# An LSTM over 512 steps: rows of x put into another basis by GpSimd, and one addition of 384 columns for a product's left sums

## The chip, the core and the metric

The kernel runs on one core of a Trainium2 chip. TensorE (PE) multiplies, with its weight loads (PEld) shown apart; VectorE (DVE) and ScalarE (ACT) do the elementwise work; GpSimd (POOL) does some elementwise work and issues some transfers; SyncE (SP) issues most of the transfers. The metric is the device time in microseconds (us), and it is compared as the median of several runs.

## The reference

For 32 sequences of 512 steps with 512 features, the output is `x + lstm(x)`:

```
xW = x @ Wx + b                       # 512 features -> 4 gates of 512
a = xW[t] + prev_h @ Wh
i, f, o = sigmoid(a[0]), sigmoid(a[1]), sigmoid(a[2]);  g = tanh(a[3])
next_c = f * prev_c + i * g
next_h = o * tanh(next_c)
```

All of it is float32. `prev_h @ Wh` must be done step after step. `x @ Wx` does not depend on the state and can be done ahead of the steps that use it.

## The kernel before, in words

**Rows.** Eight steps make a row: `load_row` (L321) brings a row of x into a tile of 128 partitions by 8 steps by 4 feature chunks by 32 sequences, over SP's queue. There are 64 rows. Seven buffers take them in turn.

**A step.** `h_part` (L870) multiplies the state with Wh in 64 matmul instructions and adds into two PSUM banks that already hold xW of that step. `cell` (L901) then runs on ACT and DVE: sigmoids and tanh (L911 to L913), the new c (L914 to L916), tanh of it (L917), h (L918) and its transposition `ht` (L919), for which the next step's `h_part` waits. While the cell runs, PE works on products for later rows of `x @ Wx`.

**x @ Wx by fast products.** Rows are taken in groups of four (`NSB` = 14 groups, rows 6 to 61) and multiplied by a scheme of 26 products of sums, in place of 32 products. An operand of such a product on the left is either a half row itself or a "node", which DVE makes from rows and other nodes (`make`, L509; the addition is at L512). Each of these products is done by an inner scheme with 2 by 2 blocks and seven block products. A left block is `a(g, e)`: `g` the earlier or later four steps, `e` one of two feature chunks. Four of the seven need a left sum, which DVE makes with four additions of 128 columns (`push_sums`, L498; additions at L540 to L543): products 5, 6, 7 and 3. Products 1, 2 and 4 take a block as it is (`left`, L545). The first rows (1 to 3) are done by the inner scheme alone, with the same four additions in `inner_sums` (L442, at L446 to L449), rows 4 and 5 by a scheme of 14, and the last two rows again by the inner scheme alone.

**Windows.** Each step has one window `v`. In order of the program: `h_part`; `announce`, which describes the jobs (products) of the next five windows; `evacuate` and `run_due`, which put ACT's and DVE's work on the results into their queues; `products(v)`, which gives PE the inner products of several jobs (five or six of them in a window on the average); `fetch(v)`, which issues the loads for later windows; `load_xw(k + 3)` on POOL's queue; `cell`; and the copies of xW into PSUM (`seed_first` L855 and `seed_last` L861, whose copies are at L859 and L865). `run_due` (L466) picks DVE's elective work from a list with due windows: an entry that is not due yet goes in only where its columns plus 160 fit into the room of the window. A due entry goes in regardless.

**xW on its way.** ACT first fills a buffer with the bias (`fill_bias`, copy at L832). POOL then issues a transfer that adds xW from DRAM to it (`load_xw`, L836), and one step later ACT copies it into PSUM. After each cell, POOL adds x to h for the output (`put_step`, L977).

**What sets the order around the change.** POOL has one queue: for a step, the transfer of L836 and then the addition of L977, which waits for `ht`. DVE has one queue: the window's evacuations, sums and nodes come ahead of the cell's operations. The rows of a group are loaded in four consecutive windows, eight windows ahead of the group. A buffer of a node is free again when the last product that reads it has been issued, by `job.release` in `products` (L588), at inner product 4.

Of the kernel before, what the change touches and what calls it, by code (L numbers as in the profile page):

```python
# [14 lines left out]
P = 128  # L15
# [267 lines left out]
def kernel(  # L283
# [155 lines left out]

    def inner_sums(a, s):  # L442

        v = nc.vector
        return [s[:, g] for g in range(4)], [
            lambda: v.tensor_add(s[:, 0], a(1, 0), a(1, 1)),  # L446
            lambda: v.tensor_sub(s[:, 1], s[:, 0], a(0, 0)),
            lambda: v.tensor_sub(s[:, 2], a(0, 0), a(1, 0)),
            lambda: v.tensor_sub(s[:, 3], a(0, 1), s[:, 1]),  # L449
        ]  # L450

    def block(src):

        return lambda g, e: src[:, 4 * g : 4 * g + 4, e]
# [30 lines left out]
    def node(sb, v):  # L485

        if v < 2 * sb.scheme.mo:
            return raw_block(sb.row + v // 2, v % 2)
        return nodes[sb, v]

    def node_done(sb, v):
        if v < 2 * sb.scheme.mo:
# [5 lines left out]
    def push_sums(job, sb, n):  # L498
        mo, a_ops, a_of = sb.scheme.mo, sb.scheme.a_ops, sb.scheme.a_of

        def want(v):
            if v < 2 * mo or (sb, v) in node_uses:
                return
            how, a, b = a_ops[v - 2 * mo]
            want(a)
            want(b)
            node_uses[sb, v] = sb.scheme.node_uses[v]

            def make():  # L509
                dst = nodes[sb, v] = node_free.pop(0)  # L510
                fn = nc.vector.tensor_add if how == "add" else nc.vector.tensor_sub
                fn(dst, node(sb, a), node(sb, b))  # L512
# [11 lines left out]
        s = job.sums = [None] * 4  # L524

        def push_sum(i, fn):
            def go():
                s[i] = spool.tile([P, 4, B], F32, name=f"s{i}_{sb.at}_{n}", tag=f"s{i}", bufs=(4, 6, 4, 4)[i])
                fn(nc.vector, block(node(sb, a_of[n])))

            push(
                job.w + i,
                P,
                go,
                lambda v: v + 1 >= job.w + i
                and (a_of[n] < 2 * mo or (sb, a_of[n]) in nodes)
                and (i % 2 == 0 or s[i // 2] is not None),
            )

        push_sum(0, lambda v, a: v.tensor_add(s[0], a(1, 0), a(1, 1)))  # L540
        push_sum(1, lambda v, a: v.tensor_sub(s[1], s[0], a(0, 0)))
        push_sum(2, lambda v, a: v.tensor_sub(s[2], a(0, 0), a(1, 0)))
        push_sum(3, lambda v, a: v.tensor_sub(s[3], a(0, 1), s[1]))  # L543

    def left(a, s, sums):  # L545
        if s in (1, 2, 4):
            return a(*{1: (0, 0), 2: (0, 1), 4: (1, 1)}[s])
        return sums[{5: 0, 6: 1, 7: 2, 3: 3}[s]]

# [38 lines left out]
    def products(v):  # L588
        for late, ss in ((4, (4,)), (2, (7,)), (0, (1,)), (1, (6,)), (0, (5,)), (1, (5,)), (3, (2, 3))):
            job = jobs.get(v - late)  # L590
            for s in ss if job and job.w < LATE_AT[0] else ():
                if s != 5 or job.w5 == v:
                    product(job, s)
                if s == 4:
                    job.release()
        for late, parts in enumerate(LATE_PLAN):
            job = jobs.get(v - late)
            for s, part in parts if job and job.w >= LATE_AT[0] else ():
                product(job, s, part)
                given[0] += 1  # L600
# [399 lines left out]
    def prepare(v):  # L1000

        job = jobs.get(v)
        ops = []
        if job is None or job.w >= PAIR_AT:
            return ops
        i, j = job.kind
        for k in range(2):
            if (i, k) not in head_sums:
                if (i, 0) not in head_sums:
                    both = spool.tile([P, 2, 4, 4, B], F32, name=f"s_h{i}", tag="sums", bufs=2)  # L1010
                head_sums[i, k], more = inner_sums(block(raw_block(i, k)), both[:, k])
# [15 lines left out]
    def describe_half(job, h, js):  # L1027
        row = LATE_ROW + 1
        if not late_half:

            def begin():
                f = free.pop(0).rearrange("p k (g t b) -> p k g t b", g=8, t=2)
                for k in range(2):
                    made, more = inner_sums(half_block(raw_block(row, k), h), f[:, k, 0:4])
# [4 lines left out]
            for m in range(8):  # L1039
                push(  # L1040
                    job.w - 3 + m / 4,
                    P // 2,
                    lambda m=m: begin() if m == 0 else half_ops.pop(0)(),
                    lambda v, m=m: v >= job.w - 3 and (len(half_ops) == 8 - m or m == 0),
                )
        job.factors = lambda s: half_factors(row, h, js, late_half)(s)
        job.finish = finish_late(job, row, (h, js))
# [3 lines left out]
    def describe_late(job, j):  # L1051
        def make(i):
            def begin():
                if not late_pairs:
                    assert len(node_free) == NODES
                    node_free.clear()
                    late_pairs.extend(node_pairs)
                tt_[i] = late_pairs.pop(0).rearrange("p m t e b -> p (m t e b)").rearrange("p (n c) -> p n c", c=C)
                ops.extend(t_sums(i))
                ops.pop(0)()  # L1060

            ops = []
# [13 lines left out]

        if isinstance(j, tuple):
            describe_half(job, *j)
            return
        for i in (j, NJ + j):  # L1080
            if i not in RESIDENT:
                make(i)
        if job.w == LATE_AT[0]:

            def both():
                f = free.pop(0).rearrange("p k (g t b) -> p k g t b", g=4, t=4)
                for k in range(2):
                    head_sums[LATE_ROW, k], more = inner_sums(block(raw_block(LATE_ROW, k)), f[:, k])
                    late_ops.extend(more)
                late_ops.pop(0)()  # L1090

            for m in range(8):
                push(
                    job.w - 2 + m / 4,
                    P,
                    lambda m=m: both() if m == 0 else late_ops.pop(0)(),
                    lambda v, m=m: v >= job.w - 2 and (len(late_ops) == 8 - m or m == 0),
                )
# [7 lines left out]
    def describe(job, sb, n):  # L1106
# [10 lines left out]
        job.factors = lambda q: [(left(block(node(sb, left_of)), q, job.sums), right(q))]  # L1117
        job.finish = finish_product(job, sb, n)
        job.release = lambda: node_done(sb, left_of)
        push_sums(job, sb, n)  # L1120

    again = [i for i in range(8) if i not in RESIDENT][1::2]

    def fetch(v):

# [21 lines left out]
            load_row(PAIR_ROW + v - NJ)  # L1147
        if rest < MO and 0 <= sb < NSB:
            load_row(HEAD // ROW + MO * sb + ROWS_AT[rest])

    with tc.manual_schedule():
        warm = work.tile([P, G, P], F32, name="warm", tag="s")
        nc.scalar.activation(warm[:, 0], c_init, AF.Sigmoid)
        for m in range(10):
# [124 lines left out]
```

## Time and profile before

| what | value |
| --- | --- |
| median of 3 runs | 3079.63 us (3079.49 to 3079.68) |
| span of the profiled execution | 3077.3 us |
| around the span (median less span) | 2.3 us |
| PE busy | 3069.2 us |
| DVE busy | 2284.0 us |
| ACT busy | 1981.0 us |
| POOL busy | 810.4 us |
| granted TensorE clock | 1.000 |

The page gives the busy time of each engine first, then the span in 40 slices, the transfers, the chain of work that ended last, and groups of instructions. A group's row has the line, engine and operation, the tiles (out<-in) with their shapes and its count, then its busy time, the mean nanoseconds of one, and the engine's idle time just before them with what ended it. A row of the timeline has the start, the duration, the engine, the line, the operation and the tiles, and in brackets the idle time of the engine before it.

### The profile page before, as it was taken

The page shows a single profiled execution, that of the slowest core. Times are in us where ns is not written, and L with a number is a line of the kernel's source. Part 1 is how long each engine was busy: PE and PEld are TensorE (multiplying, and loading weights), DVE is VectorE, ACT ScalarE, POOL GpSimd, SP SyncE. Part 2 cuts the span into 40 slices and gives each one's busy share as a digit, 9 for nine tenths or more (in the row PEclk, how much of TensorE's full clock was granted, in tenths as well). Part 3 has the DMA queues.
Part 4 walks back from the last instruction along what each step waited for, and adds up shares of the span by engine and source line. Part 5 has one row for each costly group of instructions (what it writes and reads, how often), then busy time and mean ns, then how long its engine had stood idle before and what let it go on. Part 6 is the DMA issues. An engine that isn't in the chain of part 4 may idle for free.

```text
span 3077.3 us, 133753 instructions
## 1 busy us (share of the span) xinstructions
PE 3069.2 (100%) x56612; PEld 1978.0 (64%) x56612; DVE 2284.0 (74%) x6445; ACT 1981.0 (64%) x5724; POOL 810.4 (26%) x1013
## 2 busy tenths in 40 slices
PE   9999999999999999999999999999999999999999
PEld 5555555556666666666666666666666666666666
DVE  6766777777777777777777777777777777777754
ACT  2566666666666666666666666766666666666665
POOL 0122222222222222222222222222222222222331
PEclk9999999999999999999999999999999999999999
DMA  9898898988879888898888988889898898988763
GB/s 318 239 261 214 229 255 224 249 225 235 248 212 263 229 239 242 211 266 211 258 224 216 264 224 252 224 220 263 216 260 225 226 258 221 256 225 219 196 120 71
DMA packets 350647, 708.34 MB, mean 230 GB/s; under 512 B 45792, under 2 KB 118880, under 8 KB 349536
## 3 DMA queue, kind: packets, MB, share of 16 engines
q1 hardware_dynamic: 277616, 568.41, 56.3%
q0 software_dynamic: 72000, 131.10, 26.8%
q8 instruction: 445, 7.29, 1.0%
q14 instruction: 154, 1.26, 0.1%
q10 hardware_dynamic: 432, 0.27, 0.0%
HBM read 513.88 MB, written 185.73 MB: 227 GB/s over the span
## 4 chain that ended last, share of the span: by engine, by line
PE 99%; DVE 1%; DMA 0%; ACT 0%; issue 0%; ACTq 0%; DVEq 0%
PE gates L874 53%; PE acc L579 17%; PE pp L579 17%; PE p L579 6%; PE gates L888 4%; PE gates L786 1%; PE pp L786 0%; PE acc L786 0%; DMA row<-in_x_dram 0%; DVE t L760 0%; DVE c L941 0%; DVE fc L945 0%; DVE fc L939 0%; DVE ht L949 0%; DVE nodes L367 0%
## 5 line engine op out<-in xcount | busy, mean ns | idle before, releaser
L874 PE MATMUL gates<-wh_sb,ht 128*32 128x384 f32 (+1 forms) x30144 | 1723.1, 379 | 0.0
L874 PEld LDWEIGHTS gates<-wh_sb,ht 128*32 128x32 f32 x30144 | 1022.7, 110 | 704.5 <-issue 624.0
L977 POOL TENSOR_TENSOR oc<-xr,ht 128x128 f32<-128x128 f32 x509 | 385.8, 758 | 2225.9 <-DVE ht L919 2045.7
L836 POOL DMA_DIRECT2D xw<-xw x500 | 440.0, 880 | 24.3 <-ACT xw L832 4.8
L911 ACT ACTIVATE s<-gates 128x256 f32<-128x256 f32 x472 | 181.3, 384 | 344.2 <-PE gates L874 333.4
L832 ACT COPY xw<-bias_sb 128x512 f32<-128x512 f32 x500 | 316.1, 632 | 0.0
L579 PE MATMUL pp<-wb,nodes 128*32 128x256 f32 x3920 | 312.3, 379 | 0.0
L914 DVE TENSOR_TENSOR fc<-s,c 128x128 f32<-128x128 f32 x471 | 136.9, 291 | 183.4 <-ACT s L911 180.5
L623 ACT COPY pp<-pu 128x512 f32<-128x512 f32 x396 | 238.7, 603 | 52.9 <-DVE t L744 25.8
L918 DVE TENSOR_TENSOR fc<-s,ig 128x128 f32<-128x128 f32 x472 | 137.7, 292 | 177.4 <-ACT ig L917 177.4
L625 DVE TENSOR_TENSOR pp<-acc,p 128x256 f32<-128x256 f32 x396 | 169.2, 427 | 118.8 <-ACT pp L624 118.6
L913 ACT ACTIVATE s<-gates 128x128 f32<-128x128 f32 x472 | 130.9, 277 | 147.2 <-PE gates L874 147.1
L859 ACT COPY gates<-xw 128x384 f32<-128x384 f32 x468 | 221.2, 473 | 5.4 <-DVE nodes L802 5.4
L579 PE MATMUL pp<-wb,s 128*32 128x256 f32 x2656 | 211.5, 379 | 0.0
L579 PE MATMUL acc<-wb,s 128*32 128x256 f32 x2656 | 211.5, 379 | 0.0
L579 PE MATMUL acc<-wa,s 128*32 128x256 f32 x2656 | 211.5, 379 | 0.0
L579 PE MATMUL p<-wa,s 128*32 128x256 f32 x2656 | 211.4, 379 | 0.0
L917 ACT ACTIVATE ig<-c 128x128 f32<-128x128 f32 x472 | 146.2, 310 | 100.7 <-DVE c L916 62.5
L624 ACT COPY pp<-acc 128x256 f32<-128x256 f32 x396 | 143.3, 362 | 91.0 <-DVE t L744 41.2
L618 DVE TENSOR_TENSOR pu<-acc,p 128x256 f32<-128x256 f32 x396 | 164.5, 415 | 44.3 <-ACT p L615 35.4
L919 DVE STREAM_TRANSPOSE ht<-fc 128x128 f32<-128x128 f32 x472 | 147.0, 311 | 50.3 <-DVE fc L918 1.4
L615 ACT COPY p<-p 128x256 f32<-128x256 f32 x396 | 150.5, 380 | 39.9 <-PE p L579 37.8
(239 smaller groups left out, 4478.6 us busy)
## 6 DMA issues: line engine op xcount, KB each, us to landing
wb<-keep_b SPq DMA_DIRECT2D x332, 512.0 KB, 6.2
xw<-xw POOLq DMA_DIRECT2D x500, 256.0 KB, 5.6
wa<-keep_a SPq DMA_DIRECT2D x332, 384.0 KB, 5.3
xw<-t SPq DMA_DIRECT2D x420, 128.0 KB, 4.0
xw<-raw_sb SPq DMA_DIRECT2D x272, 128.0 KB, 4.0
xr<-in_x_dram SPq DMA_DIRECT2D x256, 128.0 KB, 5.4
out_dram<-oc SPq DMA_DIRECT2D x255, 128.0 KB, 4.3
row<-in_x_dram SPq DMA_DIRECT2D x63, 512.0 KB, 8.2
```

The lines of the kernel that those rows point to most:

```text
L579: nc.tensor.matmul(dst[t * B : (t + 1) * B], a[:, t % a.shape[1]], w[t // a.shape[1]] if isinstance(w, list) else w, start=s in (1, 5) and ...
L615: nc.scalar.copy(job.p5, p5[:, 0])
L618: nc.vector.tensor_add(job.pu[:, 1], job.acc, job.p5)
L623: nc.scalar.copy(job.pp[0], job.pu)
L625: nc.vector.tensor_add(job.pp[1][:, 1], job.acc, job.p5)
L832: nc.scalar.copy(xw[t], bias_sb)
L836: nc.gpsimd.dma_start(out=xw[t], in_=stored[i][a], accum_op=mybir.AluOpType.add)
L859: nc.scalar.copy(gates[t % 2][:, 0:IFG], xw[t][:, 0:IFG])
L874: nc.tensor.matmul(g[j * B : (j + 1) * B, cols], state["ht"][:, k, :], wh_sb[:, k, j, cols], start=False, stop=True, skip_group_check=True,)
L911: nc.scalar.activation(s[:, 0:2], g[:, 0:2], AF.Sigmoid)
L919: nc.vector.transpose(ht.rearrange("p q b -> p (q b)"), h)
L977: (nc.gpsimd if t < T - 3 else nc.vector).tensor_add(state["oc"][:, tt % 2], xr[t][:, tt % 2], ht)
```

## The change

A row is put into another basis in place, once, by three subtractions of GpSimd, two windows after its load has been issued. The earlier half's first chunk stays. The other three blocks become what products 7, 6 and 3 need on the left. Products 5, 4 and 2 then need a sum, and all three sums have one term in common: the block (1, 1) of the new basis. For a node, which is now stored with its two chunks one after the other, they are one addition of 384 columns with that term repeated. For a half row they are one of 256 columns and one of 128. The nodes are sums of rows in the new basis, so that they are in the new basis, too.

```
+    def change_basis(i, a=0, b=ROW):
+        h = (b - a) // 2
+        low, high = (rows[i][:, t : t + h].rearrange("p t (k e) b -> p t k e b", e=2) for t in (a, a + h))
+        sub = nc.gpsimd.tensor_sub
+        sub(high[:, :, :, 0], low[:, :, :, 0], high[:, :, :, 0])
+        sub(high[:, :, :, 1], high[:, :, :, 1], high[:, :, :, 0])
+        sub(low[:, :, :, 1], low[:, :, :, 1], high[:, :, :, 1])
+
+    def inner_sums(src, d):
+        h = src.shape[1] // 2
+        first = src[:, :, 0].rearrange("p (g t) b -> p g t b", g=2)
+        base = src[:, h:, 1]
+        return d, [
+            lambda: nc.vector.tensor_add(d[:, 0:2], base.unsqueeze(1).to_broadcast([P, 2, h, B]), first),
+            lambda: nc.vector.tensor_add(d[:, 2], base, src[:, 0:h, 1]),
+        ]
...
+        def make_sums():
+            d = job.sums = spool.tile([P, 3, 4, B], F32, name=f"d_{sb.at}_{n}", tag="d", bufs=6)
+            if left_of < 2 * mo:
+                for op in inner_sums(node(sb, left_of), d)[1]:
+                    op()
+            else:
+                flat = node_flat(sb, left_of)
+                nc.vector.tensor_add(
+                    d.rearrange("p i t b -> p i (t b)"),
+                    flat[:, 3 * P :].unsqueeze(1).to_broadcast([P, 3, P]),
+                    flat[:, 0 : 3 * P].rearrange("p (i c) -> p i c", i=3),
+                )
+        push(
+            job.w,
+            3 * P,
+            make_sums,
+            lambda v: v + 1 >= job.w and (left_of < 2 * mo or (sb, left_of) in nodes),
+        )
...
     def left(a, s, sums):
-        if s in (1, 2, 4):
-            return a(*{1: (0, 0), 2: (0, 1), 4: (1, 1)}[s])
-        return sums[{5: 0, 6: 1, 7: 2, 3: 3}[s]]
+        if s in (1, 7, 3, 6):
+            return a(*{1: (0, 0), 7: (1, 0), 3: (0, 1), 6: (1, 1)}[s])
+        return sums[:, {5: 0, 4: 1, 2: 2}[s]]
...
-                if s == 4:
+                if s == 3:
                     job.release()
...
+    turned, changed = {}, {1, 2}
...
+        for i in turned.pop(v, ()):
+            change_basis(*i)
+        for i in list(rows):
+            if i not in changed and i:
+                changed.add(i)
+                turned.setdefault(v + 2, []).append((i, 0, ROW // 2) if i == NROWS - 1 else (i,))

     with tc.manual_schedule():
+        change_basis(1)
+        change_basis(2)
```

The last part of `fetch(v)` is where the subtractions are issued, and `load_xw` follows it on POOL's queue. Row 0 keeps its basis, and of row 63 only the first four steps change theirs; the steps left out are multiplied with Wx directly. The sums of the last two rows are pushed in four pieces, where it was eight.

More of the change, by code (lines that the diff above doesn't have):

```diff
@@ L438, in push_factors @@
             push(2 + (FACTORS_TO - 2) * i // len(ops), columns, go, lambda _, i=i: len(done) == i)
[L442 to L449, printed above, removed]
+    def change_basis(i, a=0, b=ROW):
[12 more added lines that the diff above has]
+            lambda: nc.vector.tensor_add(d[:, 2], base, src[:, 0:h, 1]),
         ]
@@ L488, in node, with node_flat @@
             return raw_block(sb.row + v // 2, v % 2)
-        return nodes[sb, v]
+        return node_flat(sb, v).rearrange("p (e t b) -> p t e b", e=2, t=ROW)
+    def node_flat(sb, v):
+        return nodes[sb, v].rearrange("p t e b -> p (t e b)")
     def node_done(sb, v):
@@ L509, in make @@
             def make():
-                dst = nodes[sb, v] = node_free.pop(0)
+                nodes[sb, v] = node_free.pop(0)
                 fn = nc.vector.tensor_add if how == "add" else nc.vector.tensor_sub
-                fn(dst, node(sb, a), node(sb, b))
+                fn(node(sb, v), node(sb, a), node(sb, b))
                 node_done(sb, a)
@@ L523, in push_sums @@
         want(a_of[n])
[L524 to L543, printed above, removed]
+        left_of = a_of[n]
+        def make_sums():
[16 more added lines that the diff above has]
+        )
     def left(a, s, sums):
-        if s in (1, 2, 4):
-            return a(*{1: (0, 0), 2: (0, 1), 4: (1, 1)}[s])
-        return sums[{5: 0, 6: 1, 7: 2, 3: 3}[s]]
+        if s in (1, 7, 3, 6):
+            return a(*{1: (0, 0), 7: (1, 0), 3: (0, 1), 6: (1, 1)}[s])
+        return sums[:, {5: 0, 4: 1, 2: 2}[s]]
     jobs = {}
@@ L1009, in prepare @@
                 if (i, 0) not in head_sums:
-                    both = spool.tile([P, 2, 4, 4, B], F32, name=f"s_h{i}", tag="sums", bufs=2)
-                head_sums[i, k], more = inner_sums(block(raw_block(i, k)), both[:, k])
+                    both = spool.tile([P, 2, 3, 4, B], F32, name=f"s_h{i}", tag="sums", bufs=2)
+                head_sums[i, k], more = inner_sums(raw_block(i, k), both[:, k])
                 ops += more
@@ L1033, in begin @@
                 for k in range(2):
-                    made, more = inner_sums(half_block(raw_block(row, k), h), f[:, k, 0:4])
+                    made, more = inner_sums(raw_block(row, k)[:, 4 * h : 4 * h + 4], f[:, k, 0:3])
                     late_half.append(made)
@@ L1037, in begin @@
                 half_ops.pop(0)()
-            for m in range(8):
+            for m in range(4):
                 push(
-                    job.w - 3 + m / 4,
-                    P // 2,
+                    job.w - 3 + m / 2,
+                    P // (1 + m % 2),
                     lambda m=m: begin() if m == 0 else half_ops.pop(0)(),
-                    lambda v, m=m: v >= job.w - 3 and (len(half_ops) == 8 - m or m == 0),
+                    lambda v, m=m: v >= job.w - 3 and (len(half_ops) == 4 - m or m == 0),
                 )
@@ L1087, in both @@
                 for k in range(2):
-                    head_sums[LATE_ROW, k], more = inner_sums(block(raw_block(LATE_ROW, k)), f[:, k])
+                    head_sums[LATE_ROW, k], more = inner_sums(raw_block(LATE_ROW, k), f[:, k, 0:3])
                     late_ops.extend(more)
                 late_ops.pop(0)()
-            for m in range(8):
+            for m in range(4):
                 push(
-                    job.w - 2 + m / 4,
-                    P,
+                    job.w - 2 + m / 2,
+                    2 * P // (1 + m % 2),
                     lambda m=m: both() if m == 0 else late_ops.pop(0)(),
-                    lambda v, m=m: v >= job.w - 2 and (len(late_ops) == 8 - m or m == 0),
+                    lambda v, m=m: v >= job.w - 2 and (len(late_ops) == 4 - m or m == 0),
                 )
@@ L1116, in describe @@
         left_of = sb.scheme.a_of[n]
-        job.factors = lambda q: [(left(block(node(sb, left_of)), q, job.sums), right(q))]
+        job.factors = lambda q: [(left(lambda g, e: block(node(sb, left_of))(g, e), q, job.sums), right(q))]
         job.finish = finish_product(job, sb, n)
```

## The prediction

> **What bounds the kernel now.** I read the page's busy times and its chain first, then busy time by stage, then single steps in the timeline.
>
> ```profile
> PE 3069.2 (100%) x56612; PEld 1978.0 (64%) x56612; DVE 2284.0 (74%) x6445; ACT 1981.0 (64%) x5724; POOL 810.4 (26%) x1013
> PE 99%; DVE 1%; DMA 0%; ACT 0%; issue 0%; ACTq 0%; DVEq 0%
> ```
>
> The chain of work that ended last is PE for 99% of the span. A busy PE need not be one that works without a pause, so the next view is single instructions of a step of five products (PE, then the end of its cell on DVE, then PE's weight loads), and the end of the cell before a step of six.
>
> ```profile
> 1505.00 0.64 PE L579 MATMUL pp<-wb,nodes 128*32 128x256 f32 x8
> 1505.43 0.64 PE L579 MATMUL acc<-wb,s 128*32 128x256 f32 x8
> ...
> 1506.72 0.64 PE L579 MATMUL p<-wa,s 128*32 128x256 f32 x8
> 1507.15 0.53 PE L874 MATMUL gates<-wh_sb,ht 128*32 128x384 f32 x4
> ```
>
> ```profile
> 1506.40 0.31 DVE L919 STREAM_TRANSPOSE ht<-fc 128x128 f32<-128x128 f32 x1
> ```
>
> ```profile
> 1506.94 0.37 PEld L874 LDWEIGHTS gates<-wh_sb,ht 128*32 128x32 f32 x8
> ```
>
> ```profile
> 1494.31 0.31 DVE L919 STREAM_TRANSPOSE ht<-fc 128x128 f32<-128x128 f32 x1
> ```
>
> ```profile
> 1495.29 0.37 PEld L874 LDWEIGHTS gates<-wh_sb,ht 128*32 128x32 f32 x8
> ```
>
> Products follow one another every 0.43 us, and the step's own matmuls begin 0.43 us after the last product: no pause. In this step `ht` is ready at 1506.71 and its first weight load begins at 1506.94, so the recurrence has a slack of 0.23 us. In the longer step it is 0.67 (1494.62 to 1495.29). PE sets the pace, but the cell is close behind.
>
> ```profile
> 0.00:100.00 100.00, 98.39 (x1636) 52.31 (x1640) 67.85 (x148) 31.90 (x87) 6.07 (x11) 1.00 0.85 293
> 100.00:2800.00 2700.00, 2700.00 (x50041) 1741.42 (x50037) 2051.40 (x5680) 1779.91 (x5023) 731.19 (x906) 1.00 0.86 237
> ```
>
> ```profile
> 3060.00:3077.30 17.30, 11.24 (x204) 7.40 (x196) 7.55 (x35) 5.75 (x28) 0.45 (x1) 0.97 0.06 17
> ```
>
> These are busy times by stage (stretch, its length, then PE, PEld, DVE, ACT, POOL, the granted clock). The clock is full, and between 100 and 2800 us PE is never idle. In the whole span it is idle for 3077.3 - 3069.2 = 8.1 us, 1.6 of them in the first 100 and 6.1 in the last 17, where the last cells have no products beside them.
>
> **The change part by part.** PE's work stays: the same seven products, blocks and columns, with other operands on the left. So a saving elsewhere gains at most the 8.1 us of idle PE, while anything that comes too late is lost in full.
>
> *DVE's sums.*
>
> ```profile
> L540 DVE TENSOR_TENSOR s<-nodes 128x128 f32<-128x128 f32 x261 | 81.7, 313 | 0.1
> ...
> L543 DVE TENSOR_TENSOR s<-nodes,s 128x128 f32<-128x128 f32 x261 | 72.6, 278 | 0.0
> L512 DVE TENSOR_TENSOR nodes<-row,nodes 128x512 f32<-128x512 f32 x99 | 65.3, 659 | 0.1
> L540 DVE TENSOR_TENSOR s<-row 128x128 f32<-128x128 f32 x117 | 33.6, 287 | 0.0
> ...
> L543 DVE TENSOR_TENSOR s<-row,s 128x128 f32<-128x128 f32 x117 | 33.0, 282 | 0.0
> ```
>
> Four additions take about 4 x 0.29 = 1.17 us. Between 128 columns (0.29) and 512 (0.66), 384 come to 0.54 and 256 to 0.41. Sums of nodes: 261 x (1.17 - 0.54) = 164 us. Sums of rows: 117 x (1.17 - 0.41 - 0.29) = 55. DVE loses some 219 us, 0.46 in each of 472 steps, and comes down to 2065, 67% of the span. On the path this is 0, because DVE holds up no PE between 100 and 2800. The trace has no addition with a repeated operand: it takes between 0.54 (as a plain one) and 1.17 us (no gain); I take 0.54, since the columns are the same in number. The nodes' additions keep their 512 columns: 0.
>
> *GpSimd's subtractions.* 63 rows by three; 56 rows belong to the 14 groups. Each has 256 columns, of which the trace shows no example; its 128 columns are these, beside DVE:
>
> ```profile
> 1517.86 0.65 DVE L744 TENSOR_TENSOR t<-t,pp 128x512 f32<-128x512 f32 x1
> ```
>
> ```profile
> 1518.03 0.45 POOL L977 TENSOR_TENSOR oc<-xr,ht 128x128 f32<-128x128 f32 x1 [4.17 <-DVE ht L919]
> ```
>
> ```profile
> 201.70 0.60 POOL L977 TENSOR_TENSOR oc<-xr,ht 128x128 f32<-128x128 f32 x1 [4.86 <-DVE ht L919]
> ```
>
> ```profile
> 201.70 0.28 DVE L541 TENSOR_TENSOR s<-s,nodes 128x128 f32<-128x128 f32 x1
> 201.90 0.55 DVE L540 TENSOR_TENSOR s<-row 128x128 f32<-128x128 f32 x1
> ```
>
> Beside L744, which reads PSUM, it took 0.45. In the second case it waited for L541, and then L540 took 0.55 where its like takes 0.28: the two engines exclude each other, and POOL held DVE for 0.27 us. So 256 columns keep DVE out for 0.27 (if that is a fixed cost) to 0.54 us (by columns), and take 0.45 to 0.45 + 0.27 = 0.72. I take 0.54 and 0.72: DVE's own additions grow with their columns, from 0.29 to 0.66. A row then costs POOL 2.2 us, and up to 3.3 with 0.36 more for each wait behind DVE (0.81 against 0.45, below); DVE can be held 3 x 0.54 = 1.6 us.
>
> The cover of that: DVE's idle time ahead of the cell, what the sums free, and PE's slack.
>
> ```profile
> L914 DVE TENSOR_TENSOR fc<-s,c 128x128 f32<-128x128 f32 x471 | 136.9, 291 | 183.4 <-ACT s L911 180.5
> ```
>
> That is 183.4 / 471 = 0.39 + 0.46 + 0.23 = 1.08 us in the short step, 1.52 in the long one. DVE works 67% of the time, so the hold is 0.67 x 1.6 = 1.07 us a row, and less, because beside an operation that reads PSUM (L744 above) POOL needed no more than its 0.45. So the mean row is just covered. What remains is the row whose subtractions meet the cell itself, where only the slack helps. In each group one row lands late:
>
> ```profile
> 1512.42 0.50 SPq L324 DMA_DIRECT2D row<-in_x_dram  x1
> ```
>
> ```profile
> DMA to landing us min/median/max: 8.2/8.2/8.2
> ```
>
> It was issued at 1512.42 and landed at 1520.6, and POOL would have turned to it after the addition at 1518.03. Its subtractions would run from 1520.6 to 1522.8, with the cell. There only the slack covers. One hold of 0.54 is 0.31 more than the short step's slack and less than the long one's; half and half that is 0.15 us, for 14 groups **2.1 us**. Bounds: 0, and 56 x (1.6 - 1.08) = 29 us.
>
> *Moved past on POOL's queue: the transfer of xW, and x + h.*
>
> ```profile
> 1500.88 0.81 POOL L977 TENSOR_TENSOR oc<-xr,ht 128x128 f32<-128x128 f32 x1 [4.52 <-DVE ht L919]
> 1501.63 0.88 POOL L836 DMA_DIRECT2D xw<-xw  x1
> ```
>
> ```profile
> 1511.49 0.47 ACT L859 COPY gates<-xw 128x384 f32<-128x384 f32 x1
> ```
>
> ```profile
> DMA to landing us min/median/max: 3.8/5.6/9.1
> ```
>
> ```profile
> L911 ACT ACTIVATE s<-gates 128x256 f32<-128x256 f32 x472 | 181.3, 384 | 344.2 <-PE gates L874 333.4
> ```
>
> xW is issued at 1501.63 and first read at 1511.49, 9.86 us later; a transfer lands after 5.6 (median) to 9.1. It is now issued 2.2 to 3.3 us later in 56 steps, so the median still lands in time (8.9), and the slowest is late by up to 2.5. In the row that lands late POOL also waits for it until 1520.6, with this transfer behind it on its queue: 2.6 us more, 11.5 after the usual issue at the median and 1.6 late. Behind ACT's copy on its queue stand the evacuations of the next window, for which DVE waits. ACT has 344.2 / 472 = 0.73 us idle ahead of its sigmoid, and PE 0.23 of slack; most of the lateness ends there. I take **1 us** in all, by the median: 14 such rows at 1.6 - 0.73 - 0.67 = 0.2 would be 2.8 in long steps, and some of ACT's work behind the copy is not waited for. Bounds: 0, and a bad case: with the slower half of the landings evenly spread from 5.6 to 9.1, those over 9.86 + 0.96 - 3.3 = 7.5 are too late even for ACT's idle time and the slack, 0.23 of all and by 0.8 on the average: 56 x 0.23 x 0.8 = 10 us. The addition of x to h (L977) starts a few tenths late at worst, since POOL's step is 0.8 + 3.3 + 0.9 = 5.0 of 5.6 us; only the output waits for it: 0.
>
> *The start.* Row 1 is changed ahead of the first sums.
>
> ```profile
> L324 SPq DMA_DIRECT2D row<-in_x_dram x1: 787/787/787, 10.5 to 10.5; - x1
> ...
> DMA to landing us min/median/max: 9.0/9.0/9.0
> ```
>
> ```profile
> 19.76 0.28 DVE L446 TENSOR_TENSOR s_h<-row 128x128 f32<-128x128 f32 x1
> ```
>
> ```profile
> 20.85 1.05 PE L579 MATMUL p<-t,s_h 128*32 128x256 f32 x16
> ```
>
> Row 1 lands at 19.5, and DVE reads it at 19.76. Now two subtractions (1.44) stand between, and the third can hold DVE for its 0.54: the first sum begins at 21.5 and ends at 21.9, so PE's product begins at about 22.0, 1.15 later; its second half needs the sum of the row's other half, and waits some 0.3 more. That is **1.5 us**, and nothing hides it, since PE's next work stands behind that product. Bounds: 0 (two subtractions of 0.45 and a sum of 0.41 end at 20.8) and 2.7 (three of 1.08, 0.41 for the sum, and the 0.3).
>
> *The rest.* Buffers of nodes come free one window earlier (at product 3): no later than before, 0. Fewer pieces for the last two rows: PE's idle 6.1 us there are the cell's own chain, with no sums in it: 0.
>
> **Sum.** 0 + 2.1 + 1 + 1.5 = 4.6 us on the profiled execution's span of 3077.3, so 3081.9; with the 2.3 us around the span, 3084.2 against the median of 3079.63. About 0.2%, 6.2 us, is what a measurement of this kernel tells from no change. The forecast lies within it.
>
> **The rivals.** *The subtractions hold up the cell (slower).* Place: DVE ahead of L914 in the 56 steps. If DVE is shut out for the whole operation of POOL, a row holds 0.67 x 3 x 0.72 = 1.45 us, 0.37 above the cover of 1.08: 56 x 0.37 = 21 us, with the start and xW 3103. It decides from (6.2 - 2.5) / 56 = 0.07 us a row above the cover. For it: the slack of 0.23. Against it: at 201.90 L540 ended at 202.45, having taken its 0.28 from 202.17, and POOL ended at 202.30, so the hold ended 0.13 earlier. The Trainium skill, page "SBUF — State Buffer", section "Who interferes with whom", says that whoever of VectorE with two inputs in SBUF and GpSimd starts first keeps the shared pair for the whole instruction, while the other is fully blocked. The trace agrees on the blocking and shows a shorter hold; by that rule the time is this rival's. Chance 0.20.
>
> *xW comes late (slower).* The upper bound of 10 us in place of 1: 3079.6 + 1.5 + 2.1 + 10 = 3093. For it: 0.8 us between the slowest landing and its reader. Against it: the median has 4.3. Chance 0.14.
>
> *The sums are not shorter.* If an addition of 384 columns took 1.17 us, nothing would be freed, the cover would be 0.62, and 56 x (1.07 - 0.62) = 25 us would be added to 1.5 and 1: 3107. Chance 0.04.
>
> *Faster.* Shorter sums at the start (four operations for eight) and less DVE work at the end could take back the 1.5 us and a little of the idle PE: some 3078. More than 0.2% would need 6.2 of the 8.1 us, most of them in the last 17 us, where the cell's own chain stands. Chance 0.03.
>
> **How the numbers follow.** Forecast 0.55, the three slower rivals 0.38, other stalls of the two close queues 0.04, faster 0.03. So within 0.2% 0.55, slower 0.42, faster 0.03. The range reaches from just below no change, 3079, to the first rival, 3103; inside it lies the second, outside the third and the worse halves of the others. The forecast's own range is 3080 to 3086.
>
> **What would show it.** DVE's busy time near 2065 and longer operations beside POOL's; POOL's three subtractions near 0.72 each when alone; PE's product after the first sums at 22.0; PE idle or behind 0.43 us a product only in some of the 56 steps. Wrong would make it: subtractions of over 1 us, many weight loads of L874 that wait for `ht`, or ACT's L859 waiting for the transfer in many steps.

## The result, and the profile after

The median rises from 3079.59 us (3079.49 to 3079.68) to 3093.73 us (3093.24 to 3093.94): 14.1 us, a ratio of 1.0046 with a 95% interval of 1.0032 to 1.0060. The span of the profiled execution grows from 3077.3 to 3091.8 us. The kernel has become slower by 0.46%. This is inside the range of the prediction, but the forecast of 3084.2 was 9.5 us too low, and "within 0.2%" was wrong.

From the page of the kernel after, the busy times and the chain by engine:

```profile
PE 3072.9 (99%) x56612; PEld 2020.5 (65%) x56612; DVE 2182.7 (71%) x5408; ACT 1981.1 (64%) x5724; POOL 950.4 (31%) x1202
...
PE 95%; DVE 2%; DMA 2%; SPq 0%; ACT 0%; issue 0%; POOL 0%; DVEq 0%
```

DVE lost 101 us of work, and yet its share of the chain grew from 1% to 2%. Busy time by stage of the kernel after (columns as in the prediction):

```profile
0.00:100.00 100.00, 97.03 (x1600) 51.08 (x1604) 67.09 (x133) 30.39 (x83) 21.46 (x25) 1.00 0.85 293
100.00:2800.00 2700.00, 2690.46 (x49796) 1775.29 (x49792) 1944.85 (x4666) 1772.76 (x5002) 849.74 (x1070) 1.00 0.86 235
...
3060.00:3091.80 31.80, 25.74 (x468) 17.38 (x460) 14.18 (x66) 12.26 (x58) 1.84 (x4) 0.97 0.09 27
```

Between 100 and 2800 us, where PE was never idle before, it is now idle for 9.5 us. The end is unchanged: 6.1 us idle, as before. The clock is the same.

To see where in those 2700 us, one can take, for each of the 472 steps, the start of its first matmul of `h_part` after, less the same start before. The difference is flat for long stretches and rises at few places:

```
step   before    after    after less before
   0     46.67    48.60    1.93
  57    425.67   428.53    2.86   (+0.92)
 248   1554.21  1562.10    7.89
 249   1560.25  1569.08    8.83   (+0.94)
 440   2688.62  2702.20   13.57
 441   2694.67  2709.18   14.52   (+0.94)
 471   2871.65  2886.28   14.62
```

There are thirteen rises of 0.92 to 1.03 us, at steps 57, 89, 121 and so on to 441, one in every 32 steps, which is one in each group of four rows but the last. Thirteen by 0.94 is 12.2 us; the start has 1.93; three small rises (0.25, 0.11, 0.11) make the rest. A cost of the subtractions would come with the rows, four times in 32 steps, or with the one row that lands late. This comes once, and at a step in which GpSimd changes no row. DVE in the window ahead of step 249, from the timeline of the kernel after:

```profile
1562.33 0.28 DVE L458 TENSOR_TENSOR d<-row 128x128 f32<-128x128 f32 x1
1564.31 0.43 DVE L638 TENSOR_TENSOR pp<-acc,p 128x256 f32<-128x256 f32 x1 [1.70 <-ACT pp L637]
1564.65 1.22 DVE L773 TENSOR_TENSOR t<-t,raw_sb 128x1024 f32<-128x1024 f32 x1
1565.89 1.23 DVE L773 TENSOR_TENSOR t<-t,t 128x1024 f32<-128x1024 f32 x1
1567.04 0.28 DVE L927 TENSOR_TENSOR fc<-s,c 128x128 f32<-128x128 f32 x1
...
1568.62 0.31 DVE L932 STREAM_TRANSPOSE ht<-fc 128x128 f32<-128x128 f32 x1
```

and PE at its end:

```profile
1569.08 0.53 PE L887 MATMUL gates<-wh_sb,ht 128*32 128x384 f32 x4 [0.73 <-DVE ht L932]
```

The same window in the timeline of the kernel before:

```profile
1554.50 0.28 DVE L540 TENSOR_TENSOR s<-row 128x128 f32<-128x128 f32 x1
1556.41 0.43 DVE L625 TENSOR_TENSOR pp<-acc,p 128x256 f32<-128x256 f32 x1 [1.64 <-ACT pp L624]
1556.76 1.22 DVE L760 TENSOR_TENSOR slot<-slot,t 128x1024 f32<-128x1024 f32 x1
1557.89 0.28 DVE L914 TENSOR_TENSOR fc<-s,c 128x128 f32<-128x128 f32 x1
...
1559.48 0.31 DVE L919 STREAM_TRANSPOSE ht<-fc 128x128 f32<-128x128 f32 x1
1559.71 1.18 DVE L760 TENSOR_TENSOR slot<-t,slot 128x1024 f32<-128x1024 f32 x1
```

In both, DVE waits some 1.7 us for ACT. In the kernel before, one addition of 1024 columns then comes ahead of the cell, and the second follows behind `ht`; in the kernel after, two come ahead of it. The cell begins 1.48 us after the start of L625 before, and 2.73 us after the start of L638 after: 1.25 more. The recurrence's slack takes some 0.3 of them, and the step's start is late by the other 0.94. PE's idle 0.73 is not all of that: the rows of a product last 0.64 us, while the next matmuls otherwise start 0.43 after that product's start (both in the prediction's rows), so 0.21 of the pause counts as busy.

The pattern is the same in all thirteen windows: two additions of 1024 columns stand directly ahead of the cell there, and in no other step, and in no step of the kernel before. The chain's 2% of DMA are mostly pieces of 4 to 5 us in these windows, where the page's chain goes back from the first L773 to a transfer of weights. DVE did not wait for it: in each of the thirteen the first L773 starts 0.34 us after L638, as L458 starts 0.34 after an L457 of the same 256 columns (in the timeline further below).

Why two? `run_due` takes an entry that is not due yet where its columns plus 160 fit into the room of the window. As the code charges them, this window had 4300 - 672 (a node) - 3 x 288 (the sums that fall into it) - 416 (an evacuation) = 2348 left before, and so had the other twelve. One addition of 1024 columns is charged 1184, two are charged 2368: the second missed by 20. The three sums have become one entry of 384 columns at 544, so 2668 are left, and the second fits. The wait for ACT isn't charged at all. That is theory A: the time that the sums freed was spent again by the planner, in a window that has it only on paper. Theory B, in the expectations below, is that GpSimd's subtractions cost the time.

### The profile page after: what moved, and what is told of

Same layout as the page of the kernel before. It is cut to its first block, busy times and chain, and to the rows that moved or that the text cites. A ratio compares the mean times of both kernels' runs of the same rounds, so it can differ in the third digit from the quotient of the medians.

```text
span 3091.8 us, 132991 instructions
## 1 busy us (share of the span) xinstructions
PE 3072.9 (99%) x56612; PEld 2020.5 (65%) x56612; DVE 2182.7 (71%) x5408; ACT 1981.1 (64%) x5724; POOL 950.4 (31%) x1202
## 4 chain that ended last, share of the span: by engine, by line
PE 95%; DVE 2%; DMA 2%; SPq 0%; ACT 0%; issue 0%; POOL 0%; DVEq 0%
PE gates L887 51%; PE acc L592 17%; PE pp L592 16%; PE p L592 5%; PE gates L901 4%; DMA wb<-keep_b 1%; DMA wa<-keep_a 1%; DVE t L773 1%; PE gates L799 0%; DVE raw_sb L773 0%; SPq L341 0%; DMA row<-in_x_dram 0%; DVE slot_h L773 0%; PE acc L799 0%; PE pp L799 0%
## 5 line engine op out<-in xcount | busy, mean ns | idle before, releaser
L887 PEld LDWEIGHTS gates<-wh_sb,ht 128*32 128x32 f32 x30144 | 1048.5, 110 | 692.1 <-issue 590.9
L990 POOL TENSOR_TENSOR oc<-xr,ht 128x128 f32<-128x128 f32 x509 | 375.6, 738 | 2031.1 <-DVE ht L932 1873.2
L592 PE MATMUL pp<-wb,d 128*32 128x256 f32 x5312 | 427.7, 379 | 0.0
L592 PE MATMUL acc<-wa,nodes 128*32 128x256 f32 x3920 | 294.0, 379 | 0.0
L638 DVE TENSOR_TENSOR pp<-acc,p 128x256 f32<-128x256 f32 x396 | 169.3, 427 | 141.0 <-ACT pp L637 138.9
L592 PEld LDWEIGHTS pp<-wb,d 128*32 128x32 f32 x5312 | 193.9, 110 | 39.8
L592 PE MATMUL p<-wa,d 128*32 128x256 f32 x2656 | 214.0, 379 | 0.0
L592 PEld LDWEIGHTS acc<-wa,nodes 128*32 128x32 f32 x3920 | 154.0, 110 | 58.4
```

The source lines that it names most:

```text
L592: nc.tensor.matmul(dst[t * B : (t + 1) * B], a[:, t % a.shape[1]], w[t // a.shape[1]] if isinstance(w, list) else w, start=s in (1, 5) and ...
L638: nc.vector.tensor_add(job.pp[1][:, 1], job.acc, job.p5)
L887: nc.tensor.matmul(g[j * B : (j + 1) * B, cols], state["ht"][:, k, :], wh_sb[:, k, j, cols], start=False, stop=True, skip_group_check=True,)
L990: (nc.gpsimd if t < T - 3 else nc.vector).tensor_add(state["oc"][:, tt % 2], xr[t][:, tt % 2], ht)
```

## Experiments

### At most one long addition ahead of its time

The kernel after, in `run_due`:

```
-        i = spent = 0
+        i = spent = long = 0
...
-            if window > v and (columns + FIXED > room - spent or not ready(v)):
+            if window > v and (columns + FIXED > room - spent or (columns > 4 * P and long) or not ready(v)):
...
             spent += columns + FIXED
+            long += columns > 4 * P
```

> The changed kernel, but one call of run_due takes at most one operation of more than 512 columns that is not due yet. This moves the second addition of 1024 columns out of 13 windows, one in each group but the last, and changes nothing else on DVE's list but the two entries behind it. Theory A (the cheaper sums leave 2668 columns of room where 2348 were left, so that a second addition of 1024 columns, 1.2 us, goes in ahead of the cell): the 13 delays of 0.94 us go, 3093.7 - 12.2 = 3081.5. Theory B (GpSimd's subtractions hold DVE or make xW late): the subtractions are all there, so 3093 to 3094.

Measured: 3082.15 us (3081.03 to 3083.37), against 3079.37 before on the same chip; ratio 1.0009 (1.0000 to 1.0018). All thirteen rises are gone; by the same comparison of starts, 1.93 at step 0 and 0.27 at step 181 are left (the profiled execution was the fastest of ten, 3081.03). DVE in the same window of this kernel:

```profile
1558.45 0.43 DVE L639 TENSOR_TENSOR pp<-acc,p 128x256 f32<-128x256 f32 x1 [1.71 <-ACT pp L638]
1558.79 1.22 DVE L774 TENSOR_TENSOR t<-t,raw_sb 128x1024 f32<-128x1024 f32 x1
1559.93 0.28 DVE L928 TENSOR_TENSOR fc<-s,c 128x128 f32<-128x128 f32 x1
```

The cell is back where it was, 1.48 us after the start of L639. GpSimd's subtractions are all still there, so they are not what cost the 12 us.

### The kernel before, with 20 columns more room

```
-ROOM = 4300
+ROOM = 4320
```

> The kernel before, with ROOM at 4320 in place of 4300 and nothing else. The room left in the same 13 windows is then 2368, just what two additions of 1024 columns are charged. Theory A: a second one goes in, the cell is held up 13 times by 0.9 us or a little less, since four short sums stand in its DVE list where the changed kernel has one or two: 3079.6 + 9 to 12 = 3089 to 3092, with no work of GpSimd in it. Theory B: no change, 3079.6.

Measured: 3091.56 us (3091.40 to 3091.66); ratio 1.0039 (1.0024 to 1.0054). Thirteen rises of 0.92 to 1.09 us at the same steps, 12.4 in all. Here nothing of the change is in the kernel: four short sums, no subtraction, POOL busy for 818.2 us. DVE's timeline in this kernel, and PE's:

```profile
1562.09 0.43 DVE L625 TENSOR_TENSOR pp<-acc,p 128x256 f32<-128x256 f32 x1 [1.63 <-ACT pp L624]
1562.43 1.22 DVE L760 TENSOR_TENSOR slot<-slot,t 128x1024 f32<-128x1024 f32 x1
1563.68 1.23 DVE L760 TENSOR_TENSOR slot<-t,slot 128x1024 f32<-128x1024 f32 x1
1564.82 0.28 DVE L914 TENSOR_TENSOR fc<-s,c 128x128 f32<-128x128 f32 x1
```

```profile
1566.86 1.50 PE L874 MATMUL gates<-wh_sb,ht 128*32 128x384 f32 x16 [0.73 <-DVE ht L919]
```

The same picture as in the changed kernel, down to PE's 0.73 us. Twenty columns of room are enough to make the loss, and one long addition less is enough to take it away: theory A is shown from both sides.

### The sums alone

The kernel after, with the subtractions left out (the sums then take operands in the old basis):

```
     def change_basis(i, a=0, b=ROW):
...
-        sub(high[:, :, :, 0], low[:, :, :, 0], high[:, :, :, 0])
-        sub(high[:, :, :, 1], high[:, :, :, 1], high[:, :, :, 0])
-        sub(low[:, :, :, 1], low[:, :, :, 1], high[:, :, :, 1])
+        return
```

> The changed kernel without GpSimd's subtractions: the rows keep their basis, so that the products take wrong operands on the left and the output is not the reference's; the rest is the same. Theory A: the 13 delays stay, and only the start (1.9 us) and some 0.4 us of other delays go: 3091.4. Theory B: nothing holds DVE, 3079.6 to 3080.

Measured: 3091.18 us (3091.14 to 3091.30); ratio 1.0038 (1.0023 to 1.0053). The thirteen rises stay (0.94 to 0.98), the start's 1.93 falls to 0.1. So of the change's 14.1 us the sums make some 12 and the subtractions some 2.3, of which 1.8 are at the start. DVE's busy time, 2163.7 us, also shows what the shorter sums save without any hold by GpSimd: 120 us less than before.

### The subtractions alone: four, two and three a row

The kernel before, its sums as they were, with subtractions of GpSimd on rows 3 to 62 at the change's place; with four for each row ("a row" below; two passes over each of two blocks, which leaves the row as it was):

```
+    def there_and_back(i):
+        low, high = (rows[i][:, t : t + 4].rearrange("p t (k e) b -> p t k e b", e=2) for t in (0, 4))
+        for e in range(2):
+            for _ in range(2):
+                nc.gpsimd.tensor_sub(high[:, :, :, e], low[:, :, :, e], high[:, :, :, e])
```

> The kernel before, with its old sums, and four subtractions of 256 columns by GpSimd for each of the rows 3 to 62 at the place where the change has three; each pair of them gives the row back as it was, up to rounding. Theory A: DVE's list is as before, and the holds cost what the changed kernel shows beside its 13 delays, 0 to 2 us: 3079.6 to 3081.6. Theory B: as much as the change costs or more, since four subtractions meet a DVE that is busier: 3092 or more.

Measured: 3097.76 us (3096.08 to 3098.70); ratio 1.0061 (1.0044 to 1.0077). This is 18.4 us, and theory A had said at most 2. Thirteen rises of 0.90 to 1.15 us, one every 32 steps from step 53 to 437, make 12.1 of the 17.0 in the profiled execution. The window ahead of step 213, POOL and then DVE:

```profile
1348.88 3.22 POOL L447 TENSOR_TENSOR row<-row 128x256 f32<-128x256 f32 x4
```

```profile
1349.96 0.60 DVE L550 TENSOR_TENSOR s<-nodes,s 128x128 f32<-128x128 f32 x1
1350.48 0.81 DVE L549 TENSOR_TENSOR s<-nodes 128x128 f32<-128x128 f32 x1
1351.22 0.28 DVE L548 TENSOR_TENSOR s<-s,nodes 128x128 f32<-128x128 f32 x1
1351.43 0.82 DVE L547 TENSOR_TENSOR s<-row 128x128 f32<-128x128 f32 x1
1352.17 1.21 DVE L767 TENSOR_TENSOR t<-slot_h,t 128x1024 f32<-128x1024 f32 x1
1353.30 0.28 DVE L921 TENSOR_TENSOR fc<-s,c 128x128 f32<-128x128 f32 x1
```

Three sums are held, for 0.32, 0.53 and 0.54 us (each takes 0.28 alone), and the cell begins behind them. So the rival of the prediction, subtractions that hold up the cell, is real on this list of DVE; it is only not what happened in the changed kernel. With `range(1)` in place of `range(2)` there are two subtractions a row:

> The kernel before, with its old sums and two subtractions of GpSimd for each of the rows 3 to 62, where four cost 18.4 us. The four delays of 0.9 us came from three holds in one window, 1.4 us of DVE. With two subtractions, about 0.5 to 1.1 us of holds stand against the slack of 0.23 to 0.67 and DVE's idle time: if a hold costs only beyond the cover, 0 to 5 us, 3079.4 to 3084.5; if each hold costs its share, half of 18.4, 3088.6.

Measured: 3080.01 us (3079.69 to 3081.49) against 3079.38; ratio 1.0002 (0.9993 to 1.0011), no difference. Half of the subtractions do not cost half of 18.4. (The "four delays" of this expectation are the thirteen rises above.) With the change's own three:

```
+        sub = nc.gpsimd.tensor_sub
+        sub(high[:, :, :, 0], low[:, :, :, 0], high[:, :, :, 0])
+        sub(high[:, :, :, 1], high[:, :, :, 1], high[:, :, :, 0])
+        sub(low[:, :, :, 1], low[:, :, :, 1], high[:, :, :, 1])
```

> The kernel before, its sums as they were, with the change's three subtractions on each of rows 3 to 62, at the change's place (the products read the changed rows as if they were the old ones, so the output is not the reference's). Two such subtractions cost nothing there and four cost 18.4 us. Theory A (the changed kernel carries its three because DVE's sums became shorter, some 0.43 us a step, which is most of the 0.54 us of one hold): three on the old list of DVE are one hold more than it has room for in some steps, and cost between the two, 5 to 15 us: 3084.4 to 3094.4. Rival (only the count of subtractions on GpSimd decides, and three fit on any list): 0 to 2 us, 3079.4 to 3081.4.

Measured: 3083.36 us (3081.78 to 3085.75) against 3079.47; ratio 1.0013 (1.0004 to 1.0021). The 3.9 us lie between the two theories: more than the rival's 2, less than theory A's 5. There is a cost, most of it in seven rises of 0.2 to 0.7 us; a further 0.38 at step 0 lies ahead of the first subtraction and is none of theirs. At the largest, step 243 with 0.71, three holds on DVE come ahead of and in the cell, and `ht` is ready at 1527.15, but PE's wait ends with ACT's copies of xW at 1527.30, whose transfer was issued behind the subtractions. So the prediction's second rival shows here too, by 0.15 us in one step.

### More subtractions on the changed kernel

The kernel of the first experiment (one long addition), with the first subtraction of rows above 2 made three times, five a row:

```
-        sub(high[:, :, :, 0], low[:, :, :, 0], high[:, :, :, 0])
+        for _ in range(3 if i > 2 else 1):
+            sub(high[:, :, :, 0], low[:, :, :, 0], high[:, :, :, 0])
```

> The changed kernel with at most one long elective operation, and five subtractions of a row by GpSimd in place of three (the first one there, back and there again; rows 1 and 2 as they were). What covers the holds is the DVE time that the sums gave up: two holds more are 1.07 us more of DVE, and 1.6 us more on POOL's queue ahead of the transfer of xW, in 56 steps. Theory A': the cover is used up by three, so that most of the 13 groups show delays as in the kernel before with four subtractions: 3082 + 5 to 15 = 3087 to 3097. If GpSimd's work is hidden whatever it is: 3082.

Measured: 3105.00 us (3103.19 to 3106.63); ratio 1.0084 (1.0069 to 1.0100), 22.9 us above the 3082.15 of three a row, and more than the 5 to 15 expected. The timeline of this kernel shows the cell itself held, for 0.81 in place of 0.28 us:

```profile
1546.88 1.21 DVE L775 TENSOR_TENSOR slot_h<-slot,slot_h 128x1024 f32<-128x1024 f32 x1
1548.01 0.81 DVE L929 TENSOR_TENSOR fc<-s,c 128x128 f32<-128x128 f32 x1
```

With `range(2)`, four a row:

> The changed kernel with at most one addition over 512 columns that is not due in a call (3082.2 us), and the first subtraction of each row made twice, so four a row (that block's second pass spoils it, so the output is not the reference's). Five cost 22.9 us more there. Theory A (DVE's list decides how many holds fit, and the shorter sums make room for nearly one): four fit nearly as three did on the old list, 2 to 10 us over 3082.2: 3084 to 3092. Rival (the count on GpSimd decides, and four cost 18.4 us on any list): 3098 to 3103.

Measured: 3092.05 us (3091.33 to 3094.96) against 3079.47; ratio 1.0043 (1.0029 to 1.0056), 9.9 us above three a row. That is at the upper edge of what theory A gave, and 6 us below the rival's 3098 to 3103. The six runs side by side, with DVE's busy time over that of the same sums without subtractions (2284.0 us for the old ones, 2163.7 for the new), divided by the 60 or 63 rows:

```
sums   a row   DVE busy   held, us a row   cost of the rows, us
old      2      2296.4        0.21           0.6
new      3      2181.0        0.27           0.9   (3082.15 - 3079.37 - 1.93)
old      3      2319.7        0.60           3.9
new      4      2203.1        0.63          10.8   (9.9 more)
old      4      2338.1        0.90          18.4
new      5      2223.1        0.94          23.7   (22.9 more)
```

The runs stand in the same order by cost as by the time for which DVE is held, while the same count on GpSimd costs 0.9 or 3.9, and 10.8 or 18.4, by DVE's list. The cost is nearly nothing up to 0.3 us a row and rises steeply from 0.6. The rows with 0.60 and 0.63 differ most (3.9 and 10.8), so the mean hold is not all of it; which step the hold meets counts, too, and that was not taken apart. The new sums make room for less than one subtraction more.

One more rival for the runs with four and five a row is an xW that comes late, since its transfer stands behind the subtractions on POOL's queue. Most of PE's waits for a step there do end with ACT's copy of xW into PSUM and not with `ht` (9.3 of 11.9 us with four on the old list). But in the window above that copy ends at 1355.13 and `ht` at 1355.12: the copy stands behind the cell's tanh on ACT's queue, and both wait for the held cell. ACT's own wait ahead of the copies for the transfer is 2.5 us in that whole run, and 11.2 us in the run with three on the new list, whose rows cost only 0.9. So it is the hold, and not the transfer, that makes most of these costs.

### The start

The kernel of the first experiment, with row 1 loaded ahead of the later part of row 0, and row 1's three subtractions made by DVE:

```
+    load_row(1)
     load_row(0, 4, 8)
-    load_row(1)
...
-        change_basis(1)
...
+        change_basis(1, engine=nc.vector)
```

> The changed kernel with at most one long elective operation in a call of run_due, and with a shorter start: row 1 is loaded ahead of row 0's second half, and DVE makes row 1's three subtractions (0.42 us each) just ahead of its sums. Theory A (all that is left of the loss is the start): the 1.9 us of the start go, 3079.6 give or take 0.7, as before the change. If the rest of the 2.8 us by which the version with one long operation is slower is not the start, 3081 or more.

Measured: 3080.64 us (3079.55 to 3081.49) against 3079.38; ratio 1.0004 (0.9995 to 1.0013). The rise at step 0 falls from 1.93 to 0.75 us. The time lies between the two that were expected (up to 3080.3, or 3081 and more), so the start is most of what was left and not shown to be all of it. This version keeps the change, with row 1's subtractions on DVE, and its interval holds 1: no difference from the kernel before is shown. None of these versions is faster than before, and little was to be won: PE had 8.1 us of idle time to begin with.

## Why the prediction was wrong on the size

That the result lies between 3079 and 3103 is luck. The upper end came from subtractions that hold up the cell, and the delay that was measured has another cause, in a term that was put at 0.

**DVE's sums: the step that failed.** "On the path this is 0, because DVE holds up no PE between 100 and 2800" reads the old list of DVE and supposes that the new one is the same list with gaps. It isn't: the sums' columns are also what `run_due` subtracts from the room. With 320 columns less charged it fills the window up again, thirteen times ahead of a cell whose window had its free time taken by a wait for ACT. That is 12.2 of the 14.1 us. The same supposition stands in the cover, where "what the sums free" is put down as time that stays free; it does only in windows that the planner does not refill. The row that would have told it was in the trace of before, one L760 ahead of the cell and one behind it; the code beside it has the room that was 20 columns short of the second.

**How much the sums free.** Predicted 219 us, measured 120 (the sums alone). The mistake is in "Four additions take about 4 x 0.29 = 1.17 us". In the prediction's rows of before at 201.70 and 201.90 the second addition starts 0.20 us after the first, while one lasts 0.28 alone: they overlap, and four take 3 x 0.20 + 0.28 = 0.88. One of 384 columns takes 0.55 where GpSimd holds nothing up, near the 0.54 taken, and 256 with 128 take 0.34 + 0.28 = 0.62 from the first start to the last end. So 261 x (0.88 - 0.55) + 117 x (0.88 - 0.62) = 117 us, close to what was measured. A repeated operand costs nothing that these rows show. The sums of nodes without subtractions (the sums alone):

```profile
L543 DVE TENSOR_TENSOR d<-nodes 128x384 f32<-128x384 f32 x261 | 145.0, 555 | 0.1
```

The groups of the kernel after, whose means contain the holds:

```profile
L545 DVE TENSOR_TENSOR d<-nodes 128x384 f32<-128x384 f32 x261 | 153.0, 586 | 0.1
...
L457 DVE TENSOR_TENSOR d<-row 128x256 f32<-128x256 f32 x117 | 58.4, 499 | 0.0
L449 POOL TENSOR_TENSOR row<-row 128x256 f32<-128x256 f32 x62 | 57.1, 921 | 4.9
...
L447 POOL TENSOR_TENSOR row<-row 128x256 f32<-128x256 f32 x62 | 47.4, 764 | 58.7 <-DMA row<-in_x_dram 58.7
L448 POOL TENSOR_TENSOR row<-row 128x256 f32<-128x256 f32 x62 | 47.3, 763 | 4.9
...
L458 DVE TENSOR_TENSOR d<-row 128x128 f32<-128x128 f32 x117 | 38.5, 329 | 0.0
```

**GpSimd's subtractions: right in mechanism and price, less in effect.** Forecast 0.72 us alone and a hold of 0.54. One row in the timeline of the kernel after, POOL and then DVE:

```profile
1538.36 0.73 POOL L447 TENSOR_TENSOR row<-row 128x256 f32<-128x256 f32 x1
1539.17 0.73 POOL L448 TENSOR_TENSOR row<-row 128x256 f32<-128x256 f32 x1
1539.98 1.02 POOL L449 TENSOR_TENSOR row<-row 128x256 f32<-128x256 f32 x1
```

```profile
1539.06 0.69 DVE L757 TENSOR_TENSOR raw_sb<-pp,raw_sb 128x512 f32<-128x512 f32 x1 [0.63 <-PE pp L592]
...
1539.99 0.41 DVE L457 TENSOR_TENSOR d<-row 128x256 f32<-128x256 f32 x1
1540.33 0.82 DVE L458 TENSOR_TENSOR d<-row 128x128 f32<-128x128 f32 x1
```

L458 takes 0.82 where it takes 0.28 alone: a hold of 0.54. The operation beside it that reads PSUM (L757) is not held. But the mean row holds DVE for (2182.7 - 2163.7) / 63 = 0.30 us, not up to 1.07: "DVE works 67% of the time, so the hold is 0.67 x 1.6 = 1.07 us a row" took all of DVE's work as work that can be held, and the rows that read PSUM only as a reason for some less. The 2.1 us for the row that lands late came to at most 0.5, the three small rises. Against the rival that DVE is shut out for the whole operation of POOL: L458 ended at 1541.15, so its own 0.28 began at 1540.87 if all of it lies behind the hold, and L449 ended at 1541.00. Read so, the hold ended 0.13 us earlier, as at 201.90 in the trace of before. The Trainium skill, page "SBUF — State Buffer", section "Who interferes with whom", says that a VectorE instruction with two inputs in SBUF contends with a GpSimd instruction that reads SBUF, and these rows agree. The other half of the rule in the prediction, that the pair is kept for the whole instruction (the page has this for two inputs in SBUF in its section "SBUF: two separate sides"), is not what these rows show, read in that way.

**xW: 1 us forecast, nothing seen.** ACT waited for it 14 times, 7.9 us in all, and none of the thirteen rises follows such a wait by less than three steps. From the groups of the kernel after:

```profile
L872 ACT COPY gates<-xw 128x384 f32<-128x384 f32 x468 | 221.5, 473 | 13.7 <-DMA xw<-xw 7.9 <-DVE nodes L815 5.3
```

**The start: 1.5 forecast, 1.93 measured.** The timeline of the kernel after:

```profile
21.45 0.42 DVE L457 TENSOR_TENSOR s_h<-row 128x256 f32<-128x256 f32 x1 [1.23 <-POOL row L448]
21.50 0.97 POOL L449 TENSOR_TENSOR row<-row 128x256 f32<-128x256 f32 x1
...
21.93 0.64 PE L592 MATMUL p<-t,s_h 128*32 128x256 f32 x8 [0.31 <-DVE s_h L457]
22.50 0.29 DVE L458 TENSOR_TENSOR s_h<-row 128x128 f32<-128x128 f32 x1 [0.62 <-POOL row L449]
22.71 0.42 DVE L457 TENSOR_TENSOR s_h<-row 128x256 f32<-128x256 f32 x1
...
23.19 0.64 PE L592 MATMUL p<-t,s_h 128*32 128x256 f32 x8 [0.61 <-DVE s_h L457]
```

The first sum begins at 21.45 and PE's product at 21.93, near the forecast (21.5 and 22.0), but by luck: the hold that was forecast for the first sum did not come, and in its place POOL starts late, at 19.88, since the row was issued 0.7 us later than before and landed 0.3 later. Where POOL starts at 19.55, in the run with four a row on the new sums, the first sum begins at 21.12 and PE's product at 21.60. The second half had been put at "some 0.3 more". It needs the second L457, which depends on no third subtraction, but L458 does, and it stands ahead of L457 on DVE's queue and waits there for L449 until 22.50.

**Of the rivals,** none came true in the changed kernel: the xW rival and the sums that are not shorter are out by the lines above, and the subtractions hold up the cell only with more of them, or on the old list of DVE. The case that did come true, a planner that spends the freed time at a bad place, was not among them.

## What to carry to other kernels

Where an order is made by a program from costs, a cheaper operation changes the order and not only its own time: run the planner's arithmetic on paper for the windows that are nearly full, and look for those with a wait that it doesn't count. Price a run of short operations by the distance of their starts, not by the sum of their durations. And work on a side engine that blocks another is free up to the slack and steep behind it: with the old sums two subtractions for each row cost nothing that could be told from no change, and four cost 18 us.

## What the runs showed of the hardware

Short additions on DVE overlap in the timeline: of 128 columns each lasts 0.28 us, and the next starts 0.20 after its start. GpSimd's subtraction of 256 columns takes 0.73 us alone and held up a DVE addition of 128 columns, both operands in SBUF, for 0.54 (0.82 against 0.28); an operation beside it that reads PSUM took 0.69, no longer than its like (0.68 in the mean). With five for each row of x, one that had to wait behind an addition of 1024 columns (L775 above) took 1.79 us:

```profile
1546.88 1.79 POOL L449 TENSOR_TENSOR row<-row 128x256 f32<-128x256 f32 x1
```

A repeated operand costs DVE next to nothing: 0.55 us for 384 columns where the plain ones gave 0.54 by interpolation.
